# Moving the first work of hop 1 into layer 0, and reordering bank copies and loads at the joins, in a fused two-layer graph kernel

## The chip, the cores and the metric

The kernel runs on one core of a Trainium2 chip. The metric is device time in microseconds (us) of one launch, as the median of several runs; lower is better. The engines are named as in the profile: PE is TensorE (PEld its weight loads), DVE VectorE, ACT ScalarE, POOL GpSimd, SP SyncE, which here mostly issues DMAs.

## What is computed

Two graph layers on 4096 nodes with 256 features, in float32. Cut to what matters:

```python
h = relu(layernorm(x)); x = x + gat(h, adj)            # layer 0: 4 heads, masked softmax, layernorm
h = relu(layernorm(x)); x = x + diffusion(h, adj)      # layer 1

def diffusion(X, S):                                   # two steps
    R = rows_normalized(S + I);  Xf = X; Xa = X; Z = 0
    for n in range(2):
        A = top_p_attention(Xa)                        # softmax, the top 0.9 of each row kept
        Xf = R @ Xf                                    # called a hop in the kernel
        Xa = A @ Xa
        Z = Z + Xf @ U1[n].T + Xa @ U2[n].T
    return layernorm(X + Z)
```

The change concerns the end of layer 0, where X is made, and the two hops `Xf = R @ Xf`, R being adj with a one added on the diagonal and rows divided by their sums.

## The kernel before

**Layer 0** runs 16 passes: pass k = 4 ig + h takes head h for a group ig of 1024 result nodes (`passes`, G0 = 8 blocks of 128). A pass walks over 16 pairs p of source blocks. For a pair, ACT (and DVE for p = 3 and 11) makes signs g (L369, L367), DVE makes two 0/1 masks m with two bit operations (L375, L376), and PE multiplies them with weighted features into the 8 PSUM banks `acc` (L395, 64 matmuls a pair). At the end of a pass `evacuate(k)` reads the banks with ACT (L409) and DVE (L411, L412) and returns a list of small pieces of work: `three`, `divided` and, after the last head of a group, `closing(ig)`: four `stats`, eight `close` (the block's residual addition and its statistics) and four `relu` (ReLU with the second layernorm, L482). The list goes to `later`, and the main loop takes one piece for each pair p from 2 to 12. So the pieces of `closing(0)` run in passes 4 and 5. Beside it, where k is 0, 4, 8 or 12, the loop has POOL add beta to one block of X for each pair (`lifted`, L578); a block has to have it before its `close`.

While layer 0 goes over a group's adjacency it also stores it in a second layout, adj_d, by POOL's DMA queue (L521); the hops read it back.

**A hop** makes 4 passes of 32 steps over the source blocks; the 128 steps are `order`. Each step needs three things:
- `source`: the block's rows. In hop 1 they are in X already; in hop 2 they are loaded from xf_d (L444).
- `split`: the rows split into a high part (ACT, L450) and the remainder (DVE, L451), both kept in hl, 5 buffers.
- `edge`: a 512 KB load of adjacency rows into ar (4 buffers) or, each fifth step of later passes and hops, into aru (L594), and `own`: where the step lies on the diagonal, DVE adds the identity to it (L602).

PE then multiplies in two halves s = 0, 1 of 4 matmuls each (L615, in `graph_products`): two column halves c by two parts t. The results of c = 0 lie in one PSUM tile of two banks (`mm`, called wide, c = 0 with s = 0 and 1), those of c = 1 in two tiles `acc`. After the last step of a pass `drained` copies the four banks out (L626): ACT those with s = 0, DVE those with s = 1. The next pass begins in another `mm` tile and in the `acc` tiles just copied. `mm` has 2 buffers, which other work (L720, L772) uses too. LOOK = 4: loads and splits run about 4 steps ahead of the matmuls.

Between the half steps of a hop (`pieces`) the loop over STEPS puts pieces of two generators: `fills` (projections of the new X, first blocks of the attention) and `picks` (their top-p search).

**The joins.** Hop 1's first five splits stand in `relu` of `closing(0)`; its first edges and own links in `hops`, which begins after the passes. Between step 0 of the loop and hop 2, `begin(second, 4)` loads four rows and edges beside the last attention block, and their c = 0 halves are multiplied there. Then comes `repaired`, a branch that is seldom taken, and hop 2 goes on with step 4: `hops` takes three sources and then edge 4, which lies in aru. aru shares its buffer with the weights u of `contributed` (L1098). In hop 2's half steps the loop also loads back the attention's result X, four blocks at a time (L1351), once every six half steps; `projections` transposes it (L765) and multiplies it (L754, L772).

**What orders the work.** Inside `tc.manual_schedule(engines=...)` each engine named runs its instructions in the order of the program text; in layer 0 SP is not named, so a scheduler places SP's DMAs, and it may also place an instruction of a later block earlier where its engine's order allows. [...]

Of the kernel before, what the change touches and what calls it, by code (L numbers as in the profile page):

```python
# [11 lines left out]
F32 = mybir.dt.float32  # L12
# [28 lines left out]
G0 = 8  # L41
# [15 lines left out]
def gat_then_top_p_diffusion(  # L57
# [104 lines left out]
    with tc.tile_pool(name="l0", bufs=1) as l0, tc.tile_pool(name="l0s", bufs=2) as l0s, tc.tile_pool(name="l0o", bufs=1) as l0o:  # L162
# [236 lines left out]
        def evacuate(k):  # L399
# [27 lines left out]
            return [three, divided] + (closing(ig) if h == H - 1 else [])  # L427
# [18 lines left out]
        def split(A, n):  # L446
            while A.parted < min(n, len(order)):
# [5 lines left out]
                A.parted += 1  # L453

        hop1 = hop_of(0)

        def closing(ig):
# [22 lines left out]
            def relu(i0):  # L480
                for b in range(ig * G0 + i0, ig * G0 + i0 + 2):
                    nc.scalar.activation(X[:, b, :], X[:, b, :], AF.Relu, scale=x_rs[:, b:b + 1], bias=x_nmr[:, b:b + 1])  # L482
                if ig == 0 and i0 < LOOK + 1:
                    for b in range(i0, min(i0 + 2, LOOK + 1)):
                        source(hop1, b)
                        split(hop1, b + 1)
# [53 lines left out]
        with tc.manual_schedule(engines=every):  # L540
# [22 lines left out]
            for n, (k, p) in enumerate(todo):  # L563
# [12 lines left out]
                if k % H == 0 and 2 < p < PAIRS - 1 and lifted:  # L576
# [9 lines left out]
        def edge(A, n):  # L586
            if n in A.ar or n >= len(order):
                return
            p, j = order[n]
            if S.spare is not None and n % 5 == 4:  # L590
                ar = S.spare.tile([P, G0 * P], F32R, name="aru", tag="u")
            else:
                ar = rp.tile([P, G0 * P], F32R, name="ar", bufs=4)
            nc.sync.dma_start(ar.bitcast(F32), adj_d[p, :, j, :].bitcast(F32))  # L594
            A.ar[n] = ar

        def own(A, n):
            while A.owned < min(n, len(order)):
                p, j = order[A.owned]
                if j // G0 == p:  # L600
                    block_ = A.ar[A.owned][:, ts(j % G0, P)]
                    nc.vector.tensor_tensor(block_, block_.bitcast(F32), ident, ALU.add)  # L602
                A.owned += 1

# [13 lines left out]
        def drained(hop, p, acc):  # L618
# [5 lines left out]
            for c in (1, 0):  # L624
                for s in range(KC):
                    (nc.vector.tensor_copy if s else nc.scalar.copy)(out_[:, c, s].rearrange("p b i -> p (b i)"), acc[c][s])  # L626
# [28 lines left out]
        def hops(A):  # L655

            turned = []
            for n in range(A.begun, len(order) + LOOK + 1):
                for i in range(3 if n == A.begun else 1):
                    source(A, n + 2 - (2 - i if n == A.begun else 0))  # L660
# [678 lines left out]
    for n in range(STEPS):  # L1339
# [4 lines left out]
        with tc.manual_schedule(engines=every):  # L1344
# [3 lines left out]
            for i, _ in enumerate(pieces, 2 * done):  # L1348
                if n > 0 and i % 6 == 5 and i // 6 < NB // 4:
# [109 lines left out]
```

## Time and profile before

| | |
|---|---|
| median of 3 runs | 2875.74 us (2874.88 to 2879.38) |
| the profiled execution | 2872.68 us, its span 2870.9 us |
| mean granted TensorE clock | 0.994 |
| DMA queue of SP (q1) | 146832 packets, 275.05 MB, 28.9% of 16 engines |

Stages of the span, as busy us of PE, DVE, ACT and POOL in windows:

| stage (us) | PE | DVE | ACT | POOL | DMA share |
|---|---|---|---|---|---|
| 100 to 300, layer 0 | 196.4 | 146.9 | 149.4 | 45.8 | 0.80 |
| 300 to 500, layer 0 | 197.1 | 156.1 | 158.2 | 30.1 | 0.73 |
| 500 to 700, layer 0 | 200.0 | 150.8 | 156.6 | 26.1 | 0.75 |
| 900 to 1000, hop 1 | 97.7 | 32.1 | 48.0 | 7.6 | 0.67 |
| 1400 to 1600, attention | 199.8 | 177.9 | 160.2 | 62.8 | 0.07 |
| 1800 to 2000, hop 2 | 195.4 | 75.8 | 53.2 | 0.0 | 0.67 |
| 2400 to 2600, attention | 200.0 | 194.4 | 159.3 | 126.5 | 0.12 |

How to read the profile's lines: a timeline line gives the start, the time until the last of the merged instructions ends, engine, line of the kernel, operation, written and read tiles, shapes, count, and in brackets the idle time of the engine before it and what ended that wait. A line of the list of waits gives who waited for whom, the total in us, how often, and the longest.

### The profile page before, as it was taken

The page shows a single profiled execution, that of the slowest core. Times are in us where ns is not written, and L with a number is a line of the kernel's source. Part 1 is how long each engine was busy: PE and PEld are TensorE (multiplying, and loading weights), DVE is VectorE, ACT ScalarE, POOL GpSimd, SP SyncE. Part 2 cuts the span into 40 slices and gives each one's busy share as a digit, 9 for nine tenths or more (in the row PEclk, how much of TensorE's full clock was granted, in tenths as well). Part 3 has the DMA queues.
Part 4 walks back from the last instruction along what each step waited for, and adds up shares of the span by engine and source line. Part 5 has one row for each costly group of instructions (what it writes and reads, how often), then busy time and mean ns, then how long its engine had stood idle before and what let it go on. Part 6 is the DMA issues. An engine that isn't in the chain of part 4 may idle for free. (4 is left out here: it accounts for less than half of the span.)

```text
span 2870.9 us, 51480 instructions
## 1 busy us (share of the span) xinstructions
PE 2798.5 (97%) x18777; PEld 2440.2 (85%) x18777; DVE 2169.1 (76%) x5069; ACT 1919.1 (67%) x3065; POOL 867.1 (30%) x1811
## 2 busy tenths in 40 slices
PE   5899999999999999999999999999999999999998
PEld 4899999999987788888888888667878888888887
DVE  8867878678654385888888887343574999999996
ACT  7876887779633646788777884232627778877882
POOL 6501211110000121322332221000204766666564
PEclk9999999999999999999999999999999999999999
DMA  8969587696366783000000001667991111111100
GB/s 193 243 229 222 186 232 186 242 194 226 141 227 199 237 296 104 20 20 20 24 23 20 20 20 48 217 205 234 326 349 49 31 34 39 31 31 31 41 29 25
DMA packets 190394, 376.48 MB, mean 131 GB/s; under 512 B 18224, under 2 KB 143152, under 8 KB 186032
## 3 DMA queue, kind: packets, MB, share of 16 engines
q1 hardware_dynamic: 146832, 275.05, 28.9%
q0 software_dynamic: 21504, 83.89, 12.3%
q10 hardware_dynamic: 21792, 14.11, 1.5%
q8 instruction: 152, 2.49, 0.3%
q14 instruction: 114, 0.93, 0.1%
HBM read 305.55 MB, written 113.57 MB: 146 GB/s over the span
## 5 line engine op out<-in xcount | busy, mean ns | idle before, releaser
L1088 PE MATMUL acc<-X,eT 128*128 128x256 f32 x4096 | 973.8, 383 | 3.4 <-ACT eT L1082 2.8
L1088 PEld LDWEIGHTS acc<-X,eT 128*128 128x128 f32 x4096 | 739.9, 191 | 110.5 <-ACT eT L1082 31.4
L395 PE MATMUL acc<-ut,m 128*128 128x195 bf16 (+1 forms) x8192 | 699.5, 247 | 7.0 <-DVE m L376 4.9
L395 PEld LDWEIGHTS <-m 128*128 128x128 fp8e4 x8192 | 696.1, 96 | 10.3 <-DVE m L376 6.1
L369 ACT ACTIVATE g<-sr,d_big 128x1024 uint8<-128x1024 f32 x448 | 472.8, 1136 | 6.4 <-DVE m L375 6.3
L903 ACT ACTIVATE e<-mm,nm 128x1024 f32<-128x1024 f32 x256 | 286.1, 1117 | 201.5 <-PE mm L720 197.8
L1082 ACT COPY eT<-tp 128x512 f32<-128x512 f32 x512 | 296.4, 580 | 89.5 <-PE tp L1080 89.2
L989 DVE MAX8 cand<-big 128x8 f32<-128x228 f32 (+1 forms) x1152 | 348.3, 380 | 0.0
L615 PE MATMUL mm<-ar,hl 128*128 128x512 f32 x844 | 342.7, 409 | 5.5 <-DMA ar<-adj_d 1.6
L971 DVE SCALAR_TENSOR_TENSOR big<-e,c 128x4096 f32<-128x4096 f32 x58 | 261.9, 4516 | 97.9 <-POOL c L956 67.1
L615 PE MATMUL acc<-ar,hl 128*128 128x512 f32 x844 | 329.2, 393 | 0.4 <-DVE ar L602 0.4
L927 POOL TENSOR_TENSOR sums<-sums 128x2 f32<-128x2 f32 x64 | 12.8, 200 | 1033.4 <-ACT void L910 1033.4
L1080 PE MATMUL tp<-ident,e 128*128 128x128 f32 x2048 | 306.3, 273 | 0.8 <-DVE e L1014 0.8
L1080 PEld LDWEIGHTS tp<-ident,e 128*128 128x128 f32 x2048 | 255.0, 141 | 60.2 <-PE acc L1098 1.2
L1014 DVE SCALAR_TENSOR_TENSOR e<-e,found 128x4096 f32<-128x4096 f32 x58 | 259.1, 4468 | 0.0
L375 DVE TENSOR_TENSOR m<-g,ax 128x512 uint32<-128x512 uint32 x256 | 179.5, 701 | 104.6 <-PE acc L395 92.4
L910 ACT ACTIVATE void<-e,c1x 128x2048 int8<-128x2048 f32 x128 | 257.4, 2011 | 0.9 <-DMA ar<-adj_d 0.5
L910 ACT ACTIVATE void<-e,c 128x2048 int8<-128x2048 f32 x128 | 257.4, 2011 | 0.0
L720 PE MATMUL mm<-kT,qT 128*128 128x512 f32 x512 | 198.5, 469 | 3.6 <-ACT e L903 1.9
L376 DVE TENSOR_TENSOR m<-m,ax 128x512 uint32<-128x512 uint32 x256 | 180.5, 705 | 25.9 <-DVE m L375 0.5
L615 PEld LDWEIGHTS mm<-ar,hl 128*128 128x128 f32 x844 | 159.5, 189 | 45.8 <-issue 6.9
L615 PEld LDWEIGHTS acc<-ar,hl 128*128 128x128 f32 x844 | 159.6, 189 | 36.8 <-issue 4.1
(302 smaller groups left out, 3512.3 us busy)
## 6 DMA issues: line engine op xcount, KB each, us to landing
ar<-adj_d SPq DMA_DIRECT2D x211, 512.0 KB, 4.5
adj_d<-ax POOLq DMA_DIRECT2D x32, 2048.0 KB, 7.5
ut<-uv_d SPq DMA_DIRECT2D x60, 784.0 KB, 5.6
aru<-adj_d SPq DMA_DIRECT2D x45, 512.0 KB, 4.5
ax<-in_adj_t_dram POOLq DMA_DIRECT2D x32, 512.0 KB, 17.5
x<-xf_d SPq DMA_DIRECT2D x78, 128.0 KB, 4.8
xf<-xft_d SPq DMA_DIRECT2D x64, 128.0 KB, 2.2
sr<-s_d SPq DMA_DIRECT2D x15, 512.0 KB, 4.8
```

The lines of the kernel that those rows point to most:

```text
L369: nc.scalar.activation(g[:, c, :], shared[k].sr, AF.Relu, scale=BIG, bias=d_big[:, h, j:j + 1])
L395: nc.tensor.matmul(shared[k].acc[i][:, t, :cols], m[t][:, c, ts(i, P)], shared[k].ut[j // QUARTER][:, j % QUARTER, t, :cols], start=(j == ...
L615: nc.tensor.matmul(A.acc[c][s], A.hl[m][:, t, ts(s, P)], A.ar[m][:, ts(c, 512)], start=(j == 0 and t == 0), stop=(j == NB - 1 and t == 1))
L720: nc.tensor.matmul(pm[:, h, :], q[t], kT[:, ds(h * (N // 2) + c * 512, 512)], start=(t == 0), stop=(t == 1))
L903: nc.scalar.activation(ev[:, :, c, :], r.pm[c], AF.Exp, bias=r.nm, accum_out=r.sums[:, c // 2, c % 2:c % 2 + 1])
L910: nc.scalar.activation(void, r.e[:, ts(h, N // 2)], (AF.Relu, AF.Sign)[i], bias=r.c1, scale=-1.0, accum_out=r.sums[:, h, 2 + i:3 + i])
L971: nc.vector.scalar_tensor_tensor(big, r.e, r.c3, r.e, ALU.is_le, ALU.mult, accum_out=r.low3)
L989: nc.vector.max(cand[:, s, :], big[:, edges[s]:edges[s + 1]])
L1014: nc.vector.scalar_tensor_tensor(r.e, r.e, r.t, r.e, ALU.is_ge, ALU.mult, accum_out=kept)
L1080: nc.tensor.transpose(pt[:, i, :], r.e[:, ts(4 * g + i, P)], ident)
L1082: nc.scalar.copy(eT, pt)
L1088: nc.tensor.matmul(r.acc[:, 0, :], eT[:, i, :], cur[:, j, :], start=(j == 0), stop=(j == NB - 1))
```

## The change

- `evacuate(k)` gives out hop 1's first work: the five sources and splits after pass 5 (so in pass 6), the four edges after pass 6, the four own links after pass 9 (so in pass 10). The splits leave `closing`. `edge` and `own` move up in the text, so that they are known there.
- Beta additions of pass 0 begin at pair 8 and not at pair 3; those of the other passes still at pair 3. As there are 32 in all, four more fall to pass 8 and one to pass 12.
- `drained` copies the banks (c, s) in the order (1,0), (0,0), (0,1), (1,1) and not (1,0), (1,1), (0,0), (0,1). ACT's two keep their order, DVE's two change places.
- `hops` asks for the edge of its first own step before the three sources.
- The loads of X in hop 2 begin at half step 1 and not 5, again every six.

```diff
--- before.py
+++ after.py
@@ -424,7 +424,18 @@
                     rs = rinv[:, ts(ig, G0)]
                     nc.vector.tensor_scalar(rs, rs, 1.0, None, ALU.add)
                     nc.vector.reciprocal(rs, rs)
-            return [three, divided] + (closing(ig) if h == H - 1 else [])
+            def sourced(n):
+                source(hop1, n)
+                split(hop1, n + 1)
+
+            ready = []
+            if k == H + 1:
+                ready = [lambda n=n: sourced(n) for n in range(LOOK + 1)]
+            elif k == H + 2:
+                ready = [lambda n=n: edge(hop1, n) for n in range(LOOK)]
+            elif k == 2 * H + 1:
+                ready = [lambda n=n: own(hop1, n + 1) for n in range(LOOK)]
+            return [three, divided] + ready + (closing(ig) if h == H - 1 else [])
 
         PASSES = NB // G0
         S = SimpleNamespace(spare=None)
@@ -451,6 +462,25 @@
                 nc.vector.tensor_tensor(hl[:, 1, :], src, hl[:, 0, :].bitcast(F32), ALU.subtract)
                 A.hl[A.parted] = hl
                 A.parted += 1
+
+        def edge(A, n):
+            if n in A.ar or n >= len(order):
+                return
+            p, j = order[n]
+            if S.spare is not None and n % 5 == 4:
+                ar = S.spare.tile([P, G0 * P], F32R, name="aru", tag="u")
+            else:
+                ar = rp.tile([P, G0 * P], F32R, name="ar", bufs=4)
+            nc.sync.dma_start(ar.bitcast(F32), adj_d[p, :, j, :].bitcast(F32))
+            A.ar[n] = ar
+
+        def own(A, n):
+            while A.owned < min(n, len(order)):
+                p, j = order[A.owned]
+                if j // G0 == p:
+                    block_ = A.ar[A.owned][:, ts(j % G0, P)]
+                    nc.vector.tensor_tensor(block_, block_.bitcast(F32), ident, ALU.add)
+                A.owned += 1
 
         hop1 = hop_of(0)
 
@@ -480,10 +510,6 @@
             def relu(i0):
                 for b in range(ig * G0 + i0, ig * G0 + i0 + 2):
                     nc.scalar.activation(X[:, b, :], X[:, b, :], AF.Relu, scale=x_rs[:, b:b + 1], bias=x_nmr[:, b:b + 1])
-                if ig == 0 and i0 < LOOK + 1:
-                    for b in range(i0, min(i0 + 2, LOOK + 1)):
-                        source(hop1, b)
-                        split(hop1, b + 1)
             return [lambda i=i: stats(i) for i in range(0, G0, 2)] + [lambda i=i: close(i) for i in range(G0)] \
                 + [lambda i=i: relu(i) for i in range(0, G0, 2)]
 
@@ -573,7 +599,7 @@
                     products(k, p, ms.pop(n))
                 if n in rest:
                     rest[n]()
-                if k % H == 0 and 2 < p < PAIRS - 1 and lifted:
+                if k % H == 0 and (2 if k else 7) < p < PAIRS - 1 and lifted:
                     b = lifted.pop(0)
                     nc.gpsimd.tensor_tensor(X[:, b, :], X[:, b, :], beta_r, ALU.add)
                 if 1 < p < PAIRS - 3 and later:
@@ -583,25 +609,6 @@
         passing.close()
         ps2 = ctx.enter_context(tc.tile_pool(name="ps2b", bufs=2, space=PSUM))
         ps1 = ctx.enter_context(tc.tile_pool(name="ps1b", bufs=2, space=PSUM))
-        def edge(A, n):
-            if n in A.ar or n >= len(order):
-                return
-            p, j = order[n]
-            if S.spare is not None and n % 5 == 4:
-                ar = S.spare.tile([P, G0 * P], F32R, name="aru", tag="u")
-            else:
-                ar = rp.tile([P, G0 * P], F32R, name="ar", bufs=4)
-            nc.sync.dma_start(ar.bitcast(F32), adj_d[p, :, j, :].bitcast(F32))
-            A.ar[n] = ar
-
-        def own(A, n):
-            while A.owned < min(n, len(order)):
-                p, j = order[A.owned]
-                if j // G0 == p:
-                    block_ = A.ar[A.owned][:, ts(j % G0, P)]
-                    nc.vector.tensor_tensor(block_, block_.bitcast(F32), ident, ALU.add)
-                A.owned += 1
-
         def graph_products(A, m, s, halves=(0, 1)):
             j = order[m][1]
             if j == 0 and s == 0:
@@ -621,9 +628,8 @@
             room = S.big if last else S.l1e.tile([P, N], F32, name="stage", tag="e1")
             out_ = room[:, :N // 2].rearrange("p (c s b i) -> p c s b i", c=2, s=KC, b=4)
             rows_ = room[:, ds(N // 2, N // 2)].rearrange("p (b d) -> p b d", b=G0)
-            for c in (1, 0):
-                for s in range(KC):
-                    (nc.vector.tensor_copy if s else nc.scalar.copy)(out_[:, c, s].rearrange("p b i -> p (b i)"), acc[c][s])
+            for c, s in ((1, 0), (0, 0), (0, 1), (1, 1)):
+                (nc.vector.tensor_copy if s else nc.scalar.copy)(out_[:, c, s].rearrange("p b i -> p (b i)"), acc[c][s])
 
             def stored():
                 for c in range(2):
@@ -656,6 +662,8 @@
 
             turned = []
             for n in range(A.begun, len(order) + LOOK + 1):
+                if n == A.begun:
+                    edge(A, n)
                 for i in range(3 if n == A.begun else 1):
                     source(A, n + 2 - (2 - i if n == A.begun else 0))
                 edge(A, n)
@@ -1346,7 +1354,7 @@
             filling, picking = fills(n, G, found, blocks), picks(n, found, blocks)
             done = 0 if n else NB - G0 - LOOK
             for i, _ in enumerate(pieces, 2 * done):
-                if n > 0 and i % 6 == 5 and i // 6 < NB // 4:
+                if n > 0 and i % 6 == 1 and i // 6 < NB // 4:
                     g = i // 6
                     nc.sync.dma_start(cur[:, ts(g, 4), :], xa_d[ts(g, 4)].rearrange("b p d -> p b d"))
                 if (n == 0 or i > 10) and i // 2 % NB != NB - 2:
```

## Prediction: what the change does to the time

> **What bounds the kernel now.** I read the page first, then the list of waits with TensorE as the waiter, then timelines around each wait, then a table of busy time in chosen windows.
>
> ```profile
> span 2870.9 us, 51480 instructions
> PE 2798.5 (97%) x18777; PEld 2440.2 (85%) x18777; DVE 2169.1 (76%) x5069; ACT 1919.1 (67%) x3065; POOL 867.1 (30%) x1811
> ```
>
> PE is idle for 2870.9 - 2798.5 = 72.4 us in all, and its steady groups run at one pace. So the kernel is bound by PE, and an edit that removes no PE work can gain only from these idle stretches (the chain of waits on the page shows DVE because of the tail). Who ends them:
>
> ```profile
> PE acc L395 <- DVE m L376: 4.9, 5, 2.7
> PE mm L615 <- DMA aru<-adj_d: 3.6, 2, 1.9
> ...
> PE tp L765 <- DMA X<-xa_d: 1.9, 1, 1.9
> ...
> PE mm L615 <- DVE stage L626: 1.4, 1, 1.4
> ```
>
> Columns: total us, times, longest. The largest rows of this list (hT, hb, 33.7 us) are the prologue, which the diff leaves alone. The others name every place that the diff touches. Two layer-0 places in the timelines of PE, DVE and SP:
>
> ```profile
> 138.13 0.32 SPq L594 DMA_DIRECT2D ar<-adj_d  x1
> 141.89 0.29 DVE L602 TENSOR_TENSOR ar<-ar,ident 128x128 fp32r<-128x128 f32 x1 [3.88 <-DMA ar<-adj_d]
> 142.84 3.32 PE L395 MATMUL acc<-ut,m 128*128 128x195 bf16 x37 [2.74 <-DVE m L376]
> 332.61 0.76 DVE L451 TENSOR_TENSOR hl<-X,hl 128x256 fp32r<-128x256 f32 x2 [3.61 <-ACT hl L450]
> 338.50 2.81 PE L395 MATMUL acc<-ut,m 128*128 128x195 bf16 x31 [0.54 <-DVE m L376]
> ```
>
> The reader sees an own link of hop 1 standing in DVE's queue early in layer 0, holding the masks behind it for 3.88 us until its load lands, and PE idle 2.74 us for those masks. At 332 us a split holds DVE for 3.61 us in the same way. Hop 2's start, in windows (PE busy, clock, DMA):
>
> ```profile
> 1810.50:1813.90 3.40, 1.55 (x7) 1.00 0.93 343
> 1813.90:1817.30 3.40, 3.40 (x10) 0.50 1.00 351
> 1817.30:1820.70 3.40, 1.47 (x8) 1.00 1.04 383
> 1820.70:1824.10 3.40, 3.40 (x14) 0.50 1.04 394
> ```
>
> Each window with PE under half busy is followed by one at half clock, so an idle stretch there costs more than itself. The join of pass 2 to pass 3 of hop 1:
>
> ```profile
> 1035.80 0.59 ACT L626 COPY stage<-mm 128x512 f32<-128x512 f32 x1
> 1036.02 0.69 DVE L626 COPY stage<-acc 128x512 f32<-128x512 f32 x1 [4.54 <-PE acc L615]
> 1036.63 0.68 DVE L626 COPY stage<-mm 128x512 f32<-128x512 f32 x1
> 1036.96 0.39 PE L615 MATMUL acc<-ar,hl 128*128 128x512 f32 x1
> ```
>
> There PE goes straight on into the bank that DVE freed at 1036.71.
>
> **What the Trainium skill says.** The page "TensorE: Matmul & The Clock Gate" (What's actually happening) has a free-running window of 3413 ns after which the clock halves when TensorE idled; the trace agrees with 3.4 us stretches at 0.50, but it shows them after windows that were still 43% to 46% busy, not wholly idle. "VectorE: DVE Perf Modes" (Two Vector instructions with no wait between them) says that the second SBUF read interface is shared with GpSimd; the trace agrees: a mask operation takes 1.21 us beside beta additions and 0.68 us without. "DMA: Bandwidth & Descriptors" (Issuing engines are not separate DMA queues) says that all DMAs share 16 engines; here a 128 KB load lands in 2.1 us at 1807.6 and needs some 3.6 us at 1809.6, behind a 512 KB load.
>
> **The change, part by part** (against the profiled run: 2872.68 us, span 2870.9; the median of the three runs shown is 2875.74, and the difference found is taken off that). Where each instruction stands comes from the built order of both kernels on each engine; the order of SP's layer-0 loads hardly changes, so hop 1's first four edges load at 138 us in both.
>
> 1. Own links. The three additions L602 that stood in DVE's queue at 141.89, 146.04 and 147.45 now stand in pass 10, after the loads have landed (by 147.6), as does the fourth, from hop 1's start. The 3.88 us wait goes; without it the mask of 142.10 ends near 139 us, before PE wants it at 142.84 - 2.74 = 140.10. Gain 2.74. The four at 0.29 us each lie in DVE's waits for PE (about 1.2 us a pair late in a pass): nothing; uncovered they would be 1.2.
>
> 2. Splits. In pass 5 they stand behind two ReLUs on ACT, which had waited for scales. PE idle there: 0.54 + 1.06 + 0.54 = 2.14. Now one split an item in pass 6. There ACT runs ahead: its first copy falls after eight sign operations (359.94 + 8 x 1.04 = 368.3), and DVE asks after the mask that ends at 371.0. So no new wait: gain 2.14. If ACT were late, DVE has 0.9 us of idle time a pair to cover it; bound 0 to 2.14.
>
> 3. Beta additions. Five of twelve leave pass 0. They ran on POOL from 104.21 and 107.07 to 117.5, at 1.05 us, beside DVE masks of 1.02 to 1.23 us (0.68 later). About 2 us of DVE time comes back before 117, so the wait of 0.87 us at 118.15 goes: gain 0.87 (bounds 0.4 and 0.87). Four go to pass 8, one to pass 12. The last of pass 8 falls on the evacuation at 488 us, as one does at 309.84 before: there L375 took 1.45 us and PE waited 0.69 us. At 488 DVE has the first bank ready at 489.25, about 1.0 us before PE asks, and 0.77 are taken: cost 0.1, bounds 0 and 0.7.
>
> 4. Order of the bank copies, at eight pass ends. The second DVE copy of the shared bank pair waits for ACT's (965.99 waits until ACT ends at 965.96). So putting it first on DVE moves it from 1036.63 only to 1036.42, 0.21 earlier, and moves the other (acc) from 1036.02 to about 1037.03, ending 1.0 later. Gain where PE waits for the pair: 0.2 of 1.38 at 870.71, 0.2 each at 1098.26, 2033.43 and 2157.89, nothing at 966.74: 0.8 together. Cost where PE runs on without filler: at 1036.96 acc is free at 1037.72 and not 1036.71, so 0.8; the same at 2095.79, where a DMA wait of 1.71 at 2111.12 takes up half or more: 0.4. At 870, 966, 1941 and 2033 other matmuls stand between, so nothing. Net cost 0.4; bounds: gain 0.8, cost 5 (0.85 at six ends).
>
> 5. Hop 2's start. The load of aru now stands on SP ahead of the last stores xa_d and z_d, ahead of the branch of the repair. It can issue when the last contribution ends (1803.2) and takes 3.7: landed at 1807. But SP passes the end of the branch only when all its lanes have landed (it stood there till 1807.4, for z_d), and the two stores now share the DMA engines with 512 KB: I take 0.7 later (0 to 1.5). The xf loads then land at 1810.3 to 1811.5, the third split ends at 1812.1, the own link at 1812.7, PE starts aru at 1812.75, not 1812.97, after 1.6 us idle. That is under half a window, so I expect no half clock: the two loads' 16 matmuls end at 1816.4, not 1818.51. X, issued two row loads and two edges earlier (1810.6, not 1812.43) with no aru ahead, follows one edge: 1810.2 + 3.7, and 1.7 more: 1815.6. It is in time; the 1.93 us wait and the second half-clock stretch go. Transposes end 1817.3, edge 6 lands near 1817.3 and needs its own link: 0.4 idle, its matmuls end 1819.6. Before they ended at 1824.79: gain 5.2. Bounds: 1 (X late, both half clocks stay) and 6. The seven further X loads only move by four half steps; no wait is seen on them before.
>
> Sum: -2.74 - 2.14 - 0.87 + 0.1 + 0.4 - 5.2 = -10.45; 2875.74 - 10.45 = 2865.3, taken as 2865.5.
>
> **The rivals.**
> A, the forecast: 2865.5; with the bounds of parts 3 to 5 without the extremes, 2862 to 2869.
> B, a wait takes the place of the one removed at hop 2's start: SP's wait at the branch grows with aru's landing, X or edge 5 comes last, one half-clock window stays. For it: DMA at 0.93 to 1.04 there. Against: aru leaves that queue. Gain there 1: -6.25, 2869.5.
> C, layer 0 gives back: DVE waits for ACT's copies in pass 6 (or for signs) as it did in pass 5, and beta beside the evacuation costs 0.7. For it: 3.61 us once before. Against: ACT's lead above. -5.65 becomes -2: 2869.
> D, the bank order costs 0.85 at six ends and hop 2 gains 2.5: -5.65 + 5.1 - 2.5 = -3.05, 2872.7. Against: filler at four ends.
> E, slower: the seven later X loads pass in front of edges that then come last. DMA share is 1.0 from 1813.9 to 1827.5, and 512 KB takes some 1.6 us; if each of seven makes PE wait that long, 11.2 is lost, and part 5 gains nothing: -5.25 + 11.2 = +6, 2881.7. It decides as soon as the edges' lead falls under 1.6 us. Against: PE waits for no edge between 1824 and 2111 before, with the same eight loads in the stream.
>
> **How the numbers follow.** A 0.62, B 0.17, C 0.08, D 0.06, E 0.07. What can be told from no change is 0.2%, 5.75 us: below 2870.0 is faster. Faster: 0.61 of A, 0.11 of B, 0.06 of C, 0.01 of D: 0.79. Slower: E, 0.07. The same: 0.14. The range 2860.5 to 2871.5 takes in A with all gains at their upper bound, B and C, and 1.7 us for a half-clock window in the tail (0.50 at 2824.2), whose phase may fall otherwise; D and E stay out.
>
> **What would show it.** Right: no PE wait at 118, 142 or 338 to 343; L602 in pass 10 without a wait; clock 1.00 after 1800; a new wait of 0.8 of PE for a DVE copy of acc at the third pass end of hop 1. Wrong: hl copies awaited in pass 6, PE waiting for aru or X by 1.8 us again, waits on ar after 1824.

## The result and the profile after

| | us |
|---|---|
| before, median of 7 runs | 2875.74 |
| after, median of 7 runs | 2866.90 |
| ratio after to before | 0.9968, 95% interval 0.9956 to 0.9980 |
| profiled execution, before and after | 2872.68 and 2866.9 |

One of the seven runs after was slow (2915.34 us at a granted clock of 0.944, where the others have 0.995 or 0.996); without it the median is 2866.36 us, and the ratio is taken without it.

The time fell by 8.8 us of the medians, by 5.8 us between the two profiled executions. The head of the page after:

```profile
span 2865.1 us, 51492 instructions
...
PE 2795.3 (98%) x18777; PEld 2436.3 (85%) x18777; DVE 2169.1 (76%) x5069; ACT 1918.8 (67%) x3065; POOL 865.7 (30%) x1811
```

PE's idle time went from 72.4 to 69.8 us only. The other 3.2 us are PE's busy time: the same 18777 matmuls, but fewer of them in half-clock windows (between the prologue and the end, one of 3.4 us where there had been three). Some waits are new and some longer than before; from the list of waits with PE as the waiter (total us, times, longest):

```profile
PE tp L878 <- DVE undone L1176: 4.6, 2, 3.3
...
PE mm L622 <- DMA aru<-adj_d: 2.2, 1, 2.2
...
PE acc L395 <- DVE st L412: 1.7, 2, 1.0
PE mm L622 <- ACT hl L461: 1.6, 2, 1.1
PE acc L622 <- DVE aru L482: 1.3, 1, 1.3
PE mm L622 <- ACT ob L502: 1.3, 1, 1.3
PE acc L622 <- DVE stage L632: 1.3, 2, 0.6
```

Lines of the kernel moved: the bank copies L626 are now L632, the hop's matmuls L615 are L622, the own links L602 are L482, the splits L450 and L451 are L461 and L462.

**A ledger.** Where did the time come from? For each PE matmul I took its start after minus its start before. Steps in that difference show what each place gained or lost. Noise in one place doesn't hide another in this way, but each step still holds the run-to-run noise of its own place:

| place | forecast, us | trace, us | sum so far |
|---|---|---|---|
| end of pass 0 (beta) | -0.87 | -1.19 | -1.24 |
| pass 2 (own links) | -2.74 | -2.90 | -4.15 |
| start of pass 5 | 0 | +0.34 | -3.80 |
| pass 5 (splits) | -2.14 | -3.08 | -6.88 |
| start of pass 9 (beta) | +0.1 | +1.22 | -5.66 |
| start of hop 1 | 0 | +0.42 | -5.24 |
| hop 1's pass ends | +0.4 | +0.39 | -4.85 |
| start of hop 2 | -5.2 | -3.40 | -8.19 |
| hop 2's pass ends, and the wait for aru after them | 0 | +0.8 | -7.40 |
| tail | 0 | +1.5 | -5.81 |

Steps under 0.1 us are not listed, and the start of the trace gave -0.05. The step at the start of hop 1 is +0.25 in a second execution of the changed kernel, and is not explained here.

Layer 0's two stalls are gone. The four own links stand between 539.4 and 545.9 us, the five remainders of the splits between 364.0 and 373.4, and DVE waits at none of them. PE runs through at both places, as its timelines show (no brackets means no idle time before the group):

```profile
135.81 9.35 PE L395 MATMUL acc<-ut,m 128*128 128x195 bf16 x108
```

```profile
329.82 15.39 PE L395 MATMUL acc<-ut,m 128*128 128x195 bf16 x179
```

The timeline at the start of pass 9, of PE, DVE and POOL, has a stall that was not there:

```profile
481.33 1.45 DVE L375 TENSOR_TENSOR m<-g,ax 128x512 uint32<-128x512 uint32 x1
...
481.49 0.74 POOL L604 TENSOR_TENSOR X<-X,beta_r 128x256 f32<-128x256 f32 x1
...
482.89 0.69 DVE L376 TENSOR_TENSOR m<-m,ax 128x512 uint32<-128x512 uint32 x1
483.50 0.15 DVE L411 TENSOR_REDUCE rinv<-acc 128x1 f32<-128x2 f32 x1
...
484.04 3.19 PE L395 MATMUL acc<-ut,m 128*128 128x195 bf16 x31 [0.68 <-DVE st L412]
```

Beside the beta addition on POOL the mask operation takes 1.45 us, not the 0.68 of its neighbours. That is one half of the delay. The other half comes from earlier in the pass, where POOL now makes six additions in a row and before made three (timelines of POOL and DVE):

```profile
463.08 4.97 POOL L604 TENSOR_TENSOR X<-X,beta_r 128x256 f32<-128x256 f32 x6
...
466.31 1.16 DVE L375 TENSOR_TENSOR m<-g,ax 128x512 uint32<-128x512 uint32 x1
...
467.57 1.03 DVE L376 TENSOR_TENSOR m<-m,ax 128x512 uint32<-128x512 uint32 x1
```

Before, these two masks took 0.66 and 0.69 us. From here to the end of the pass DVE has no idle time, so the 0.84 us lost here and the 0.77 lost at the last mask both reach the evacuation L411 and L412, for which PE waits. Its first bank is free 1.6 us later against PE's work than before (at 483.98 us; before at 489.25, with PE's work 6.88 us later). Before, it had been free 0.84 us ahead of PE's first use (490.09). PE loses 0.84 us at the first bank, and 0.4 more over the following banks, which DVE now frees as PE comes to them.

Hop 2's start, timelines of SP and PE:

```profile
1798.44 0.32 SPq L474 DMA_DIRECT2D aru<-adj_d  x1
1798.95 1.36 SPq L1102 DMA_DIRECT2D xa_d<-xa  x1
1800.41 0.38 SPq L1275 DMA_DIRECT2D z_d<-part  x1
1805.01 0.33 SPq L455 DMA_DIRECT2D xa<-xf_d  x1
...
1807.45 0.50 PE L622 MATMUL mm<-aru,hl 128*128 128x512 f32 x1 [1.06 <-ACT hl L461]
...
1809.29 0.50 PE L622 MATMUL acc<-aru,hl 128*128 128x512 f32 x1 [1.34 <-DVE aru L482]
```

aru is asked for early, as meant, but SP comes to the first row load behind the branch only at 1805.01. In the kernel before it came there at 1807.56, with PE's work 4.79 us later:

```profile
1807.56 0.33 SPq L444 DMA_DIRECT2D xa<-xf_d  x1
```

So SP is 2.2 us later against PE's work. SP leaves the branch when z_d has landed, and z_d, behind aru and xa_d, took 4.3 us from its issue in this execution (to 1804.7) and 2.9 before. But this execution is an odd one. In a second profiled execution of the changed kernel z_d took 3.0 us, and SP came to this load earlier:

```profile
1803.24 0.33 SPq L455 DMA_DIRECT2D xa<-xf_d  x1
```

There, with PE's work 0.34 us earlier, SP is 0.8 us later than before, and in seven altered kernels that keep the early edge, 0.8 to 1.1 us. In the execution shown PE then waits for the row's split and for the own link that stands behind two more splits. The wait for X is gone, and so are both half clocks of hop 2's start, as windows of that stage show (us, busy us of PE, PEld, DVE, ACT, POOL, then the granted clock, DMA share and GB/s):

```profile
1807.16:1810.58 3.42, 1.79 (x7) 1.26 (x8) 1.81 (x5) 1.45 (x4) 0.00 (x0) 1.00 0.93 248
1810.58:1813.99 3.41, 3.12 (x16) 2.21 (x15) 0.60 (x2) 0.41 (x1) 0.00 (x0) 1.00 1.06 375
```

The join of pass 2 to pass 3 of hop 1, timelines of PE and DVE:

```profile
1030.83 0.69 DVE L632 COPY stage<-mm 128x512 f32<-128x512 f32 x1 [4.94 <-ACT stage L632]
...
1031.15 0.39 PE L622 MATMUL mm<-ar,hl 128*128 128x512 f32 x1
...
1031.44 0.68 DVE L632 COPY stage<-acc 128x512 f32<-128x512 f32 x1
...
1032.18 0.50 PE L622 MATMUL acc<-ar,hl 128*128 128x512 f32 x1 [0.64 <-DVE stage L632]
1032.52 0.39 PE L622 MATMUL mm<-ar,hl 128*128 128x512 f32 x1
```

DVE's copy of acc now waits behind its copy of the shared pair, which waits for ACT's; PE waits for acc. The list counts 0.64 us, but from 1031.15 to 1032.52 two matmuls cost 1.37 us, where two steady ones take 2 x 0.227: 0.92 are lost.

In the tail, before had a half-clock window at 2824 and then a wait of 1.64 us for the search on DVE (L1168); after has no such window, so PE comes to the search earlier, waits 3.3 us for it (L1176) and has its half clock at 2834.7 instead.

### The profile page after: what moved, and what is told of

It is laid out like the page before. It is cut to its first block, busy times and chain, and to the rows that moved or that the text cites. A ratio compares the mean times of both kernels' runs of the same rounds, so it can differ in the third digit from the quotient of the medians.

```text
span 2865.1 us, 51492 instructions
## 1 busy us (share of the span) xinstructions
PE 2795.3 (98%) x18777; PEld 2436.3 (85%) x18777; DVE 2169.1 (76%) x5069; ACT 1918.8 (67%) x3065; POOL 865.7 (30%) x1811
## 5 line engine op out<-in xcount | busy, mean ns | idle before, releaser
L622 PE MATMUL mm<-ar,hl 128*128 128x512 f32 x844 | 340.7, 407 | 5.9 <-ACT ob L502 1.3
L622 PE MATMUL acc<-ar,hl 128*128 128x512 f32 x844 | 328.6, 392 | 2.3 <-DVE stage L632 1.3
L622 PEld LDWEIGHTS mm<-ar,hl 128*128 128x128 f32 x844 | 158.6, 188 | 44.9 <-issue 5.0
L622 PEld LDWEIGHTS acc<-ar,hl 128*128 128x128 f32 x844 | 158.6, 188 | 39.9 <-issue 4.9
```

Source lines behind the costliest of these rows:

```text
L622: nc.tensor.matmul(A.acc[c][s], A.hl[m][:, t, ts(s, P)], A.ar[m][:, ts(c, 512)], start=(j == 0 and t == 0), stop=(j == NB - 1 and t == 1))
```

## The experiments

Each kernel is the changed one with the edit shown. The first nine were run once each. The unaltered kernel ran from 2863.06 to 2868.51 us in one set of seven runs, so a single time says little, and the argument rests on the places in the trace. Shifts are PE's starts against the profiled execution of the changed kernel, so minus is earlier. Kernels that leave a stage alone still differ in it, which sets what counts as an effect. Hop 2's start (from 1790 to 1822) stood 1.2 us better in a second execution of the unaltered changed kernel, and 0.8 to 1.8 better in six altered ones that don't touch it; so the first profile is at the slow end there. The 1.5 us of the tail and the prologue's 0.9 come and go in the same way.

**The bank order alone undone.**

```diff
-            for c, s in ((1, 0), (0, 0), (0, 1), (1, 1)):
+            for c, s in ((1, 0), (1, 1), (0, 0), (0, 1)):
```

> The changed kernel with the old order of the bank copies, (1,0), (1,1), (0,0), (0,1). Theory 1 (the new order costs): the waits of PE for DVE's copy of acc at the third pass end of each hop (0.64 us each in the changed kernel) are gone, PE reaches the step after them 0.9 us earlier, and the four waits for the pair grow by 0.2 each; over both hops the kernel is about 1.0 us faster in its trace. Rival (the new order pays): the pair is free earlier, what waits for it moves up, and undoing it costs 0.8 us or more.

2865.01 us. PE gained 0.92 at the join of 1032 and 0.91 at that of 2089, and lost 0.2 at each of the ends where it waits for the pair. The wait for aru behind the second join took nothing of the gain: it is 2.2 us in both kernels. But a half-clock window followed it here, and 1.53 came back. Windows of this kernel (columns as above):

```profile
2099.40:2102.80 3.40, 1.39 (x6) 1.19 (x7) 1.29 (x7) 0.41 (x1) 0.00 (x0) 1.00 0.97 344
2102.80:2106.20 3.40, 3.40 (x10) 2.64 (x9) 3.17 (x6) 0.81 (x2) 0.00 (x0) 0.50 1.03 401
```

So the price of the new order is near the forecast 0.8 at the join of hop 1, and as large at hop 2's, where the forecast had 0.4. What is left of it behind hop 2's join depends on the clock.

**The edge of hop 2's first own step asked for after the branch again.**

```diff
-                if n == A.begun:
-                    edge(A, n)
```

> The changed kernel with edge 4 of hop 2 asked for after the three sources again, so that its load is issued behind the branch. Theory 1 (SP's wait at the branch is prolonged by this load, which takes back part of the gain): SP leaves the branch 2.2 us earlier, the row loads land 2 us earlier, aru itself lands last; at hop 2's first projections PE is within 1 us of the changed kernel. Rival (the early load is what the gain at hop 2's start comes from): PE waits for aru by 1.8 us or more and the clock halves once, 3 us or more are lost.

2868.08 us, with two half-clock windows in the tail, where the changed kernel's profile has one. Hop 2's start: -1.4 us, no more and no less than in kernels that keep the early edge (-0.8 to -1.8). The timelines of SP and PE tell why:

```profile
1798.71 0.34 SPq L1100 DMA_DIRECT2D xa_d<-xa  x1
...
1802.29 0.33 SPq L455 DMA_DIRECT2D xa<-xf_d  x1
...
1807.76 0.47 PE L622 MATMUL mm<-aru,hl 128*128 128x512 f32 x1 [1.69 <-DMA aru<-adj_d]
```

Without aru ahead of it the store issues in 0.34 us and SP is past the branch at 1802.29. Against PE that is 2.5 us earlier than in the first profile and 1.0 to 1.4 earlier than in the kernels that keep the early edge; this is what the load costs SP. Now PE waits 1.69 us for aru, where in those kernels it waits 1.2 to 1.6 for aru's own link. The early edge alone brought nothing that can be seen.

**The loads of X late again.**

```diff
-                if n > 0 and i % 6 == 1 and i // 6 < NB // 4:
+                if n > 0 and i % 6 == 5 and i // 6 < NB // 4:
```

> The changed kernel with the loads of X at half steps 5, 11 and so on again. Theory 1 (X was the last to come at hop 2's start): PE waits for X by 1.5 to 2.5 us before its first transposes, and with half a window idle the clock halves for 3.4 us; 2 to 4 us lost in all. Rival (with aru out of the queue X comes in time anyway): under 0.5 us lost.

2870.28 us, with a second half-clock window at 2107.7. Hop 2's start lost 2.35 us, some 3.5 against other kernels. PE waits for X, and a half-clock window follows (timeline of PE, then windows):

```profile
1814.52 1.94 PE L773 MATMUL tp<-ident,X 128*128 128x128 f32 x8 [3.16 <-DMA X<-xa_d]
```

```profile
1810.70:1814.10 3.40, 0.66 (x3) 0.19 (x1) 1.01 (x3) 0.41 (x1) 0.00 (x0) 1.00 1.05 385
1814.10:1817.50 3.40, 2.98 (x11) 2.77 (x12) 0.08 (x1) 1.48 (x3) 0.00 (x0) 0.50 1.04 394
```

Most of the gain of part 5 is the gain of the earlier X loads: 3.5 us of some 4.5. What makes up the rest was not tried alone.

**The beta additions of pass 0 put back.**

```diff
-                if k % H == 0 and (2 if k else 7) < p < PAIRS - 1 and lifted:
+                if k % H == 0 and 2 < p < PAIRS - 1 and lifted:
```

> The changed kernel with pass 0's beta additions at pairs 3 to 14 again. Theory 1 (what pass 0 gains, pass 9 gives back): 1.2 us lost in pass 0 and 1.2 us won where pass 9 begins, within 0.3 us of the changed kernel by the end of layer 0. Rival (the delay in pass 9 comes from the shifted pieces of work, not from the beta addition): 1.2 us lost and nothing won.

2865.61 us. PE lost 0.66 in pass 0 and won 1.23 at the start of pass 9. Moving the additions was worth nothing, or a loss of 0.6.

**No beta addition at the last pair of a pass.**

```diff
-                if k % H == 0 and (2 if k else 7) < p < PAIRS - 1 and lifted:
+                if k % H == 0 and (2 if k else 7) < p < PAIRS - 2 and lifted:
```

> The changed kernel with one number altered: in every pass that adds beta, the last addition stands at pair 13 and not at pair 14, so none is left beside the copies and multiplies of a pass's end; the addition dropped from passes 4 and 8 falls to pass 12. In the changed kernel PE waits 1.03 us at 308.59 and 0.68 us at 484.04 for the mask of line 412's neighbours behind such an addition. Theory 1 (the addition on GpSimd slows the pass's end on VectorE): both waits fall below 0.2, and PE stands 1.2 to 1.7 us earlier than in the changed kernel after the start of pass 9 (about 490 us); nothing else changes by more than 0.3 before 700 us. Theory 2 (VectorE's own copies set these two waits, the addition only happens to lie there): at least one of them stays at 0.6 or more. A time some 1 to 1.5 us below the changed kernel's 2866.9 if nothing later takes it back, which the other runs of this kernel make doubtful (2 us either way).

2861.83 us. PE stands 0.78 earlier from the start of pass 5 and 0.80 more from that of pass 9. The list of PE's waits had 1.7 us in two for this entry; now it has

```profile
PE acc L395 <- DVE st L412: 0.2, 1, 0.2
```

Theory 1 holds: the addition on POOL beside the end of a pass costs. At pass 9 the former kernel, with none of the four added additions, won 1.23 us, and this one, without the last, 0.80. The 0.4 between belong to the other three.

**The banks divided by tile.** VectorE copies both banks of c = 1, ScalarE both of the pair.

```diff
-            for c, s in ((1, 0), (0, 0), (0, 1), (1, 1)):
-                (nc.vector.tensor_copy if s else nc.scalar.copy)(out_[:, c, s].rearrange("p b i -> p (b i)"), acc[c][s])
+            for c, s in ((1, 0), (0, 0), (1, 1), (0, 1)):
+                (nc.vector.tensor_copy if c else nc.scalar.copy)(out_[:, c, s].rearrange("p b i -> p (b i)"), acc[c][s])
```

> The changed kernel with the bank copies divided in another way: VectorE copies both halves of c = 1 (the two tiles acc), ScalarE both halves of c = 0 (the shared pair), in the order (1,0), (0,0), (1,1), (0,1). In the changed kernel VectorE's copy of acc waits behind its copy of the shared pair, which waits for ScalarE's. Theory 1 (the second copy waits for the other engine's copy because both read one tile of two banks): with one engine for the pair no engine waits for the other; acc's two copies end at about 0.7 and 1.4 us after the pass's last product, so the waits of 0.64 us at 1032.18 and 2088.73 go (to 0.1 or less), about 0.9 us each with the clock; the waits for the pair at 865, 1092, 2027 and 2151 stay within 0.3 us of the changed kernel's (ScalarE needs two copies of 0.6 us one after the other, as now in effect). Sum 1.5 to 2.2 us less in the aligned PE starts between 860 and 2200. Theory 2 (PE waits because VectorE starts the copies late, whatever their order): the two waits stay at 0.5 or more, or the pair's waits grow by 0.5 each and eat the gain.

2863.26 us. Both stalls for acc are gone (-0.93 and -0.89), the waits for the pair became shorter (-0.22 near 865, -0.70 near 966, -0.26 near 1092). Timelines of DVE and ACT at the join:

```profile
1028.49 0.69 DVE L632 COPY stage<-acc 128x512 f32<-128x512 f32 x1 [3.63 <-PE acc L622]
...
1029.17 1.08 ACT L632 COPY stage<-mm 128x512 f32<-128x512 f32 x2 [4.88 <-PE mm L622]
...
1029.40 0.69 DVE L632 COPY stage<-acc 128x512 f32<-128x512 f32 x1 [0.22 <-PE acc L622]
```

Now each copy waits for PE alone. The Trainium skill, "PSUM — Partial Sum Buffer" (Specifications (TRN2)), says that ScalarE and VectorE can read PSUM in parallel where they don't meet in a bank; this trace agrees, with two copies of 0.69 us on DVE beside two in 1.08 us on ACT. In the kernels before and after it was the shared tile that put DVE's copy behind ACT's; that all four copies write one tile, stage, is so here too and holds nothing up. By 2115 2.0 us were lost again in hop 2, mostly in waits for ar of 1.0 at 2097 and 0.3 at 2106; the wait for aru is 2.4, against 2.2 in the changed kernel.

**Splits and own links put back.** `ready` is empty for both, and the splits stand again in `relu`.

```diff
-                ready = [lambda n=n: sourced(n) for n in range(LOOK + 1)]
+                ready = []
...
-                ready = [lambda n=n: own(hop1, n + 1) for n in range(LOOK)]
+                ready = []
...
+                if ig == 0 and i0 < LOOK + 1:
+                    for b in range(i0, min(i0 + 2, LOOK + 1)):
+                        source(hop1, b)
+                        split(hop1, b + 1)
```

> The changed kernel with two of its parts undone: hop 1's splits stand again behind the two ReLUs in pass 5, its own links stand again at the start of hop 1 (as does what the scheduler then pulls into layer 0); the early edges, beta additions, bank order and loads of X stay changed. Theory 1 (in-order queue of VectorE: the masks stand behind an operation that waits for another engine or a load): PE loses 2.1 to 3.1 us again at 330 to 345 us, at the splits. With the edges still early, the four own links find their data landed; if they are still pulled up into pass 2 or any other pass they wait at most for nothing, and PE's wait at 118 to 145 us stays away (the load, not the addition, was the price); so loss 2.1 to 3.1 in pass 5, 0 to 1.2 at hop 1's start. Theory 2 (the gains of 2.9 and 3.1 came with the beta additions and the general pace of VectorE): less than 1 us is lost at 330 to 345.

2876.44 us: all the gain of the change was lost. At the splits PE lost 3.08 us, Theory 1's upper end. In pass 2 it lost 6.54, where I had expected nothing: the own links were again placed early in layer 0, with their loads still at 137 us and after, as in the kernel before and in the changed one (from 138.1 and 137.9). Timelines of DVE and PE, and windows:

```profile
140.97 0.29 DVE L482 TENSOR_TENSOR ar<-ar,ident 128x128 fp32r<-128x128 f32 x1 [4.64 <-DMA ar<-adj_d]
```

```profile
141.92 14.28 PE L395 MATMUL acc<-ut,m 128*128 128x195 bf16 x132 [3.49 <-DVE m L376]
```

```profile
137.70:141.10 3.40, 0.73 (x9) 0.50 (x6) 0.13 (x1) 3.40 (x4) 0.00 (x0) 1.00 0.83 278
141.10:144.50 3.40, 2.58 (x16) 2.40 (x17) 3.26 (x6) 2.57 (x3) 0.00 (x0) 0.51 1.01 415
```

DVE takes its instructions in order: for 4.64 us no mask passes the waiting addition, and PE stands still for 3.49. So this part's gain is not in loading earlier but in naming the place of the addition. Here the stall filled most of one clock window, and two windows of half clock, to 147.9, were paid on top; in the kernel before a stall of 2.74 us had lain across two windows and paid nothing.

**Five steps of hop 2 begun, not four.**

```diff
-                beside.update({1: both_weights, 2: lambda: begin(second, 4), 5: lambda: split(second, 2), 6: lambda: (split(second, 4), own(second, 4))})
+                beside.update({1: both_weights, 2: lambda: begin(second, 5), 5: lambda: split(second, 2), 6: lambda: (split(second, 5), own(second, 4))})
```

> The changed kernel with five and not four steps of hop 2 begun beside the last attention block: the fifth row load and the fifth edge (in aru) are asked for there, and the fifth split stands beside the fourth. The own link of the fifth stays where it is. Theory 1 (hop 2's start is bound by what SP may issue only after the branch; the row load, its split and so aru's multiplication come 2.24 us later than forecast because SP leaves the branch later): PE's waits of 1.06 and 1.34 us at 1807 to 1809 shrink to under 0.8 together, and PE stands 1.2 to 2.4 us earlier than in the changed kernel by 1822 us. Theory 2 (the DMA engines are the bound from 1798 on: 512 KB loads at full share): what is saved at 1807 comes back as waits for the next edge or for X before 1830, and PE is within 0.7 us of the changed kernel by 1830. Because this stretch varies by some 1.5 us from run to run, only 1.5 or more counts as a gain.

2871.89 us. Neither theory: PE lost 6.1 us here, two half-clock windows (1805.7 and 1815.9) included. The fifth step's products, ahead of the branch, wait for aru, and so PE comes to the branch later (timeline of PE; then, from the view of the branch's line L1264, count, min/median/max ns and start of PE's own branch instruction):

```profile
1802.48 0.70 PE L622 MATMUL mm<-aru,hl 128*128 128x512 f32 x2 [0.89 <-SPq L1264]
1806.24 1.19 PE L622 MATMUL mm<-aru,hl 128*128 128x512 f32 x2 [3.05 <-PEq L1264]
```

```profile
L1264 PEldq COMPARE_BRANCH  x1: 3417/3417/3417, 1802.5 to 1802.5; - x1
```

On PE the branch takes 3.4 us. In the changed kernel it takes 3.5, from 1797.8, and 16 queued matmuls of 4.0 us hide it but for 0.45 us of idle time; here two were left to hide it. SP's own waits at the branch were over at 1803.0, but its next load, an edge, goes into a buffer that PE reads after the branch, and it started only at 1809.17.

**The fifth step made ready ahead of the branch, but not multiplied.**

```diff
-                beside.update({1: both_weights, 2: lambda: begin(second, 4), 5: lambda: split(second, 2), 6: lambda: (split(second, 4), own(second, 4))})
+                beside.update({1: both_weights, 2: lambda: (begin(second, 4), source(second, 4)), 5: lambda: split(second, 2), 6: lambda: (split(second, 5), own(second, 4))})
...
+            if n + 1 < STEPS:
+                edge(second, 4)
             finish(r)
             finish_scale(r)
             finish_rows(r)
+            if n + 1 < STEPS:
+                own(second, 5)
```

> The changed kernel with the fifth step of hop 2 made ready ahead of the repair branch but not multiplied there: its row is loaded and split beside the last attention block, its edge (aru) is asked for between the two last stores, its own link is added before the branch, and the order SP is given also puts the next three row loads ahead of the branch; four steps are begun as before. Theory 1 (after the branch PE waits for what SP could only issue once it had left it: row, split, own link): the waits of 1.06 and 1.34 us at 1807 to 1809 both go, what is left is the wait for the next edge (issued near 1805, some 3.7 to 4.6 us, so 0.3 to 1.2 us of wait), and PE stands 1.5 to 2.8 us earlier than in the changed kernel by 1822. Theory 2 (the branch is left when all lanes have landed, and more bytes ahead of it move it back by what they take, 0.5 MB or 1.4 us): SP leaves at 1806.4 or later relative to PE's last product before the branch, and PE gains less than 0.7 by 1822. In both cases part of a gain can be taken back near 2104, where the DMA engines run at a share of 1.0 and PE waits for aru.

2866.71 us. Hop 2's start: -2.64, some 1.4 beyond the mean of the kernels that leave it alone and 0.8 beyond the best of them. Both waits are gone. SP passed the branch 0.5 us earlier against PE than in the first profile, but 0.9 later than in the second, so Theory 2's later branch came in part. By 2050 1.0 of the gain had come back; that is no mark of this edit, since 1.2 came back there in the second execution of the unaltered kernel.

**The changed kernel again, and two combinations,** run beside the former on one chip: the last beta addition and the banks by tile together, and these two with the fifth step made ready.

> The changed kernel itself, unaltered, in the same call as the two combinations, so that they are compared on one chip. All theories: 2865 to 2868 us, ratio to the kernel before 0.9960 to 0.9980, and its waits where they were: 1.03 and 0.68 us at the starts of passes 5 and 9, 0.64 us twice at the joins, 1.1 and 1.3 us at hop 2's start, about 2.2 us for aru near 2104.

> The changed kernel with two alterations that each run alone gave time in the trace: the last beta addition of a pass at pair 13 (1.58 us in layer 0), and VectorE copying both halves of c = 1, ScalarE both of c = 0 (about 0.9 us at 1032, 0.7 at 966, 0.2 each at three other ends, 0.9 at 2089). Theory 1 (the two are independent and stand on the path): their sum up to the end of hop 1 is 1.58 + 1.6 to 2.0, the part after 2089 is lost again at 2104, where aru comes late, so the time is 2.8 to 3.8 us below the changed kernel's of this call: 2862.5 to 2864. Theory 2 (what is gained upstream goes into later waits for DMA, as at 2104): less than 1.5 us below it.

> As the former, with the fifth step of hop 2 made ready ahead of the branch as well (row, split, edge, own link, next three rows). Theory 1 (loads and PE at hop 2's start move forward together, so DMA does not take the gain back at 2104): 1.5 to 2.8 us below the former: 2860 to 2862. Theory 2 (from 2035 to 2110 the stream of edges and rows runs at the DMA engines' rate, and PE arriving earlier only waits longer for aru near 2104): within 0.8 us of the former.

| kernel | median, us | lowest to highest | ratio to before, 95% interval |
|---|---|---|---|
| before (11 runs) | 2874.48 | 2871.40 to 2877.11 | 1 |
| changed kernel (7) | 2865.16 | 2863.06 to 2868.51 | 0.9969 (0.9958 to 0.9980) |
| beta and banks (5) | 2862.25 | 2861.71 to 2863.23 | 0.9961 (0.9947 to 0.9975) |
| these and the fifth step (5) | 2861.40 | 2859.20 to 2862.34 | 0.9955 (0.9942 to 0.9969) |

Beta and banks together take 2.9 us off the changed kernel's median, at the lower end of what their sum of parts gave; the intervals of the ratios overlap, but four of the five runs lie below all seven of the changed kernel. In the trace 1.58 came in layer 0 and 2.0 in hop 1, and the gain at 2089 went at 2102, in a wait of 1.1 us for ar. The fifth step took 0.85 us more off the medians, with overlapping runs; in its trace hop 2's start gained no more than without it (-0.79 against -0.75). SP passed the branch 2.0 us later against PE than in the kernel without the fifth step, and PE now waited for the next edges. From its timeline of PE:

```profile
1804.95 0.47 PE L622 MATMUL mm<-ar,hl 128*128 128x512 f32 x1 [1.49 <-DMA ar<-adj_d]
...
1809.07 0.47 PE L622 MATMUL mm<-ar,hl 128*128 128x512 f32 x1 [1.06 <-DMA ar<-adj_d]
```

Whether it is worth anything stays open.

## Why the prediction was right

The forecast was 2865.5 us, with a range of 2860.5 to 2871.5; the change measured 2866.90 and, in a second set of runs, 2865.16. The gain was 8.8 us of the medians, where the sum had 10.45. Case A happened, with several terms off. The 5.8 us between the first two profiles are at the low end: the second profiled execution of the changed kernel is 7.9 us shorter than the one of before (2863.0 against 2870.9 us). By its steps:

1. **Own links**, -2.74: -2.90 measured. The mechanism is shown by putting them back: DVE stands at the first of them until its load lands. (The loss was larger then, 6.54, by two half-clock windows.)
2. **Splits**, -2.14: -3.08 measured, and 3.08 lost when put back. The mechanism was right; the size was read from the list of waits, which counts 0.54, 1.06 and 0.54. From start to start the three stalls cost 0.80, 1.30 and 0.80 us where a steady matmul takes 0.085, so 2.64, and two slips of 0.19 and 0.23 ahead of the first are in no list. A stall's gap is counted from the modelled end of the matmul before it, which lies 0.16 us after its successor's normal start.
3. **Beta**, -0.87 and +0.1: -1.19 and +1.22. Here a bound failed: "bounds 0 and 0.7". The slow mask was foreseen, but it was the only one of the four added additions that I priced, against a lead of DVE over PE of about 1.0 us. The lead was 0.84, and the three others had used it up. Undoing it shows that the move as a whole gained nothing; keeping the last addition clear of the pass's end gains 1.58, of which 0.44 was a cost at pass 5 that the kernel before already paid (0.78 less the 0.34 of the ledger). Those 0.34 were not forecast. In the trace the last mask operation before the evacuation, at 307.44, waits 0.46 us for PE, which it did not before; where splits and own links were put back this wait is gone and 0.38 came back. Why it arises stays open.
4. **Bank order**, +0.4: +0.39 in hop 1, as forecast. In hop 2, with 0 forecast, the join cost 0.9 and the stretch behind it ended at +0.8: the wait for aru, which was to take up half of the cost or more, grew from 1.71 to 2.23 us. The serial copies of one tile were read rightly; dividing them by tile removes the cost.
5. **Hop 2's start**, -5.2: -3.40 in the profiled run and, going by the second execution and the kernels that leave it alone, -4.1 to -5.2 usually (against the one profile of before). "I take 0.7 later (0 to 1.5)" for SP at the branch was right as a rule: 0.8 to 1.1 in eight executions. In the profiled one it was 2.2, which none of the others repeats. That this delay takes back what the early edge gives is close to the forecast too, which had PE at aru only 0.2 us earlier (1812.75, not 1812.97). The larger term, X in time and no half clock, held and is shown by moving X back.

That layer 0 came out at -5.66 against a forecast of -5.65 is luck: +1.46 of unseen costs at passes 5 and 9 stand against -1.42 of gains read too small. The tail gave back 1.5 in this profile through the phase of a clock window, for which the range had left 1.7.

Of the rivals, B was half right: SP's wait at the branch did grow, but neither X nor a half clock came of it. C's beta beside the evacuation came, and the waits for splits in pass 6 did not. D's cost of 0.85 fell at two ends, not at six. For E, in the profiled run PE waited for no edge between 1815 and 2090; and E's 1.6 us for a 512 KB load was high, since at the 394 GB/s of its windows I estimate 1.3.

## What to carry to other kernels

An operation that waits for a load on an engine that works in program order, as DVE does here, should be given its place by hand, late enough that its data is surely there; loading earlier doesn't help if the operation can drift up with it. Price a stall from start to start of the stalled engine's instructions, not by the gap in a list. Where work is moved to run beside a busy engine, add up what all of it slows from that engine's last idle time to the stage's end: here two masks in the middle of a pass had used up the lead that was to hide the last one. Before moving a load ahead of a barrier such as a branch, ask when the issuing queue gets past it: what is gained for that load can be lost by all that come after it. And profile a stage twice before explaining a size: the first profile's 2.2 us at the branch was a single case.

## What was not expected of the hardware

- The same idle time costs nothing more or 1.5 us more (1.53 found; half of a 3.4 us window would be 1.7), by its phase in the windows. "TensorE: Matmul & The Clock Gate" (What's actually happening) has the window free-running, and the traces agree: with the stall of 2.2 us at 2104 the changed kernel's window was 1.56 us busy and no half clock followed, while with 2.2 us in the kernel with the old bank order it was 1.39 busy and one did. Windows under half busy, which the prediction took for the sign of it, are not enough: besides this 1.56 a window of 1.49 us busy in the second execution (at 2829.5) was followed by full clock, and one of 1.55 in the kernel before (at 1810.5) by half.

```profile
2100.91:2104.32 3.41, 1.56 (x7) 0.94 (x6) 2.58 (x3) 0.41 (x1) 0.00 (x0) 1.00 1.00 324
2104.32:2107.74 3.42, 3.04 (x13) 2.53 (x14) 2.24 (x4) 0.81 (x2) 0.00 (x0) 1.00 1.00 378
```

- A branch on PE takes 3.4 to 3.9 us in six kernels, on ACT, DVE and SP 0.05 to 0.07. Where 13 or 16 queued matmuls (3.3 to 4.0 us) ran in that time PE was idle for 0.30 to 0.45 us, where only two did, for 3.05.
- A store of 128 KB issued on SP behind a 512 KB load held SP for 1.26 to 1.77 us in eight profiles, and for 0.34 in those where no such load stood ahead of it. The load alone doesn't decide it: with five steps begun the store behind it took 0.34, and in the kernel with beta and banks the first store took 0.34 and the second 1.29.
- From 2035 to 2130 the changed kernel's DMA share is 0.97 to 1.03 (376 GB/s from 2035 to 2070). In each of the four kernels with other bank copies the gain at hop 2's join, in this stretch, was lost again within 20 us, but not in one way: in two of them to a half-clock window behind the wait for aru, in the other two mostly to waits of 1.0 and 1.1 us for ar.
